# Context times probabilities in a two-layer cross-attention kernel: a 4x3x2 block product of twenty products in place of two Strassen-type halves of eleven

## Chip, core and metric

The kernel runs on one core of a Trainium2 chip, all in float32. The metric is the device time of one execution in microseconds (us); lower is better. TensorE is PE in the profile (PEld is its weight load), VectorE is DVE, ScalarE is ACT, GpSimd is POOL, SyncE is SP, which here only issues transfers.

## What is computed

Eight batches; each has 100 rows `x` (512 wide) and a context of 361 rows (512 wide). Three stages follow one another: a single-head cross-attention (called the first layer below), a block of two 16-head cross-attentions with layer norm in front, and an MLP. Cut to what matters:

```python
# the first layer, per batch
q, k, v = x @ w_q.T, ctx @ w_k.T, ctx @ w_v.T
x = x + alpha * (softmax(q @ k.T / sqrt(512)) @ v) @ w_o.T
# twice, with weights 1 and 2: 16 heads of 128, one more key and value (the bias ones)
h = layer_norm(x)
logits = (h @ wq + bq) @ concat(ctx @ wk + bk, bias_k).T / sqrt(128)     # per head
x = x + (softmax(logits) @ concat(ctx @ wv + bv, bias_v)) @ wo + bo      # per head
# MLP
x = x + gelu(layer_norm(x) @ w_fc1 + b_fc1) @ w_fc2 + b_fc2
```

The kernel doesn't form keys and values. It takes the queries through the key weights to 512 columns ("wide queries", held in the tile `Z`), scores them against the context itself, multiplies the probabilities with the context itself (the *mix*, which overwrites `Z`), and takes that through the value weights (`head_out`). The change concerns the mix: for each batch a matrix of 512 x 361 (the context, transposed by the way PE reads it) times 361 x 1600 (the probabilities of 16 heads x 100 rows).

## The kernel before

**Order.** `emit` walks a list of small units; each issues its instructions in turn, and rings of buffers (`Ring`) issue the loads of weights and contexts as slots come free. A scheduler then settles the order on each engine; every engine works its own queue in order. The mixes, scores, projections and outputs of neighbouring steps are woven into one another by hand (`woven`, `apart`, and the loop at the end of the function), so that PE goes from one to the other while the other engines empty what it has made. `apart` puts two units of the mix that work on the same chunk apart, with another unit between them where it can.

**Steps.** A step is (layer l, pair of batches q, group of heads g), 24 in all, and each has two batches j: 48 *units of work* per execution for the mix. The 1600 probability columns are cut into groups of 576, 512 and 512 (`ROWS`), and each group into two halves of 288 or 256 columns.

**Probabilities.** A pair of score tiles of 128 rows is exponentiated, scaled (ACT, L343) and turned by DVE in blocks of 32 x 32 (`turned`, L359, one instruction for each quarter of the keys and each 32 rows, at a lowered priority) into the tile `pT`. That tile holds nine blocks of 128 keys x half a group: six for the 3 x 2 blocks of probabilities (three blocks of keys, two halves of columns), three for sums of them. When the last quarter of the last pair is turned, `column_sums` (L817) sends the row of the bias key to DRAM and forms the sums on POOL (L822 to L825); in the very last unit on DVE.

**The mix** (`mixed`, L849, matmuls in the helper at L858). The context's 512 columns are four blocks, its 361 rows three (128, 128 and 105). For each half m of the columns there are four parts with eleven products in all, so 22 per unit of work: seven for a 2 x 2 by 2 x 2 product in Strassen's manner, with the accumulators x and z reused from product to product and read in between, and four plain ones for the third block of keys (of 105 rows). The results go into four blocks of `Z` per half: a first value is copied by ACT (L867, L870, L875, L889), three later ones are added by DVE (L878, L884, L885). So a unit of work has eight ACT and six DVE evictions.

**Context blocks.** The 20 stationary blocks of a batch (10 per half) are loaded for each layer into a tile of the ring `ctx` by five transfers (`fill_ctx`, L170 to L179): three from the input, two from a DRAM scratch `cxd`, which holds the 10 summed blocks. These are formed once, in the first layer (`ctx_sums`, L438): five POOL operations of 128 x 256 into the tile `msum` (one buffer) and two transfers out.

**The first layer.** For each batch (`layer0_units`): its context is loaded (`fill_ctx0`, two transfers; rings `ctx` for even and `ctx0` for odd batches, two slots each, so batch b + 4 takes the slot of batch b), transposed for the scores (`ctx_transposed`, which also forms sums in the tile `cT` on DVE, L467 to L469), scored, mixed (`l0_mixed`), summed (`ctx_sums`) and put out. Weights for a bias term (`wqe`) are loaded from POOL's queue (`bias_weights`, L157) and multiplied on DVE (L604) in between. `bias_vectors` (L627) loads two vectors through POOL's queue and subtracts them on DVE.

Of the kernel before, what the change touches and what calls it, by code (L numbers as in the profile page):

```python
# [19 lines left out]
P = 128  # L20
# [23 lines left out]
A11, A12, A22, A13, A23, A33, M1, M2, M3, M4 = range(10)  # L44
# [36 lines left out]
def two_cross_attentions(ctx: ExitStack, tc: tile.TileContext, a: dict, out: bass.AP):  # L81
# [16 lines left out]
    cxd = [dram.tile([P, 10 * P], F32, tag=f"cxd{b}", name=f"cxd{b}") for b in range(B)]  # L98
# [60 lines left out]
    def fill_ctx0(key, t):  # L159
        src = a["ctx_2048"][key[2]]  # L160
        t = t[:, : 3 * D].rearrange("p (k n) -> p k n", k=3)
        nc.sync.dma_start(out=t[:, :2, :], in_=src[: 2 * P].rearrange("(c p) n -> p c n", p=P))
        nc.sync.dma_start(out=t[:TS, 2, :], in_=src[2 * P :])

    def fill_ctx(key, t):
        if key[1] < 0:
            return fill_ctx0(key, t)
        src = a["ctx_2048"][key[2]]
        t = t.rearrange("p (m u n) -> p m u n", m=2, n=P)
        nc.sync.dma_start(out=t[:, :, A11, :], in_=src[:P].rearrange("p (m n) -> p m n", m=2)[:, :, :P])  # L170
        nc.sync.dma_start(
            out=t[:, :, A12:A13, :], in_=src[P : 2 * P].rearrange("p (m u n) -> p m u n", m=2, n=P)
        )
        nc.sync.dma_start(
            out=t[:TS, :, A13:A33, :], in_=src[2 * P :].rearrange("p (m u n) -> p m u n", m=2, n=P)
        )
        d = cxd[key[2]].rearrange("p (m u n) -> p m u n", m=2, n=P)
        nc.sync.dma_start(out=t[:, :, M1:, :], in_=d[:, :, 1:, :])
        nc.sync.dma_start(out=t[:TS, :, A33, :], in_=d[:TS, :, 0, :])  # L179
# [258 lines left out]
    def ctx_sums(b):  # L438

        cx = ctx0(b).rearrange("p k (m u n) -> p k m u n", m=2, n=P)  # L440
        t = work.tile([P, 2, 5, P], F32, tag="pb", name=f"msum_{b}", bufs=1)
        nc.gpsimd.tensor_tensor(t[:, :, 1], cx[:, 0, :, 1], cx[:, 1, :, 1], ALU.add)
        nc.gpsimd.tensor_tensor(t[:, :, 2], t[:, :, 1], cx[:, 0, :, 0], ALU.subtract)
        nc.gpsimd.tensor_tensor(t[:, :, 3], cx[:, 0, :, 1], cx[:, 0, :, 0], ALU.subtract)
        nc.gpsimd.tensor_tensor(t[:, :, 4], cx[:, 1, :, 0], t[:, :, 2], ALU.subtract)
        nc.gpsimd.tensor_tensor(t[:TS, :, 0], cx[:TS, 2, :, 0], cx[:TS, 2, :, 1], ALU.subtract)
        out = cxd[b].rearrange("p (m u n) -> p m u n", m=2, n=P)
        tc.keep_in_program_order(nc.sync.dma_start(out=out[:, :, 1:, :], in_=t[:, :, 1:, :]))
        nc.sync.dma_start(out=out[:TS, :, 0, :], in_=t[:TS, :, 0, :])
# [78 lines left out]
    def layer0_units():  # L528
# [21 lines left out]
        for b in range(B):  # L550
            res.append(unit(lambda b=b: l0_probs(b)))
            res += scored(b + 1)
            res.append(unit(lambda b=b: l0_mixed(b), key0("ctx", b)))
            res.append(unit(lambda b=b: ctx_sums(b), key0("ctx", b)))
            res += turned(b + 2) + normed0(b + 1)
            res += weights(b + 4)
            if b == 0:
                res.append(unit(bias_vectors))
# [258 lines left out]
    def column_sums(l, q, g, j, engine=nc.gpsimd):  # L817


        t, t3 = pTs[l, q, g, j], columns(l, q, g, j)  # L820
        nc.sync.dma_start(out=pbd[l, q * QB + j][:, slice(*ROWS[g])], in_=t3[TS : TS + 1, 2, :])
        engine.tensor_tensor(t[:, 6], t[:, 1], t[:, 0], ALU.subtract)  # L822
        engine.tensor_tensor(t[:, 7], t[:, 3], t[:, 6], ALU.subtract)
        engine.tensor_tensor(t[:, 1], t[:, 1], t[:, 3], ALU.subtract)
        engine.tensor_tensor(t[:, 8], t[:, 2], t[:, 7], ALU.subtract)  # L825
# [10 lines left out]
    def last_turned(l, q, g, j, r, m):  # L836
# [4 lines left out]
        if m:  # L841
            column_sums(l, q, g, j, nc.vector)
# [581 lines left out]
```

## Time and profile before

| | |
|---|---|
| three runs | 1990.54 median (1988.27 to 1991.58) us |
| the profiled execution | 1987.13 us, span 1985.3 us |
| granted PE clock | 0.998 |
| PE busy, mix (tiles mx, mz, my at L858) | 960 + 768 + 384 passes |
| PE busy, 0 to 60 us | 55.3 us |
| PE busy, 60 to 180 us (the first layer's batches) | 111.0 of 120 us |
| PE busy, 180 to 1772 us (the two 16-head layers) | 1569.6 of 1592 us |
| PE busy, 1772 us to the end (last outputs, MLP) | 206.7 of 213.3 us |
| DVE busy, the same four stretches | 13.1, 64.1, 1095.3, 106.7 us |
| POOL busy, the same four stretches | 18.9, 39.1, 580.1, 61.7 us |

A float32 product shows as two matmul instructions (passes), each with its weight load. A pass's listed duration runs into the next one's, since matmuls are pipelined; the pace is read from when the next work starts. In rows of the form `L885 DVE TENSOR_TENSOR Z<-my,Z 128x256 f32<-128x256 f32 x64 | 27.0, 421 | 2.1 <-PE my L858 0.7` the columns are line, engine, operation, output and inputs, shapes, count, busy time in us, mean ns of one, then the idle time just before them and what ended most of it. In tables by stretch the columns are the stretch, its length, and the busy time and count of PE, PEld, DVE, ACT and POOL, then granted clock, share of the transfer engines and GB/s.

### The profile page before, as it was taken

To read this page: it belongs to the slowest core of one execution; us is meant where nothing else is said; L and a number is where in the kernel's file an instruction comes from. 1 tells how busy PE (TensorE), PEld (TensorE's weight loads), DVE (VectorE), ACT (ScalarE), POOL (GpSimd) and SP (SyncE) were. 2 spreads that over 40 slices of the span, in tenths; PEclk is the share of its full clock that TensorE was granted. 3 is DMA by queue.
4 is the path that set the end of the run, shared out by engine and by line. 5 is a ranking of instruction groups with operands and counts; after the bars stand their busy time and mean duration, and the time that the engine had idled before them with its cause. 6 is when DMAs were issued, how large, how long until landed. Compare 5 with 4: busy or idle time off the path is not lost.

```text
span 1985.3 us, 31528 instructions
## 1 busy us (share of the span) xinstructions
PE 1942.6 (98%) x10991; PEld 1788.5 (90%) x10991; DVE 1279.1 (64%) x3555; ACT 761.3 (38%) x2018; POOL 699.8 (35%) x1147
## 2 busy tenths in 40 slices
PE   9999999999999999999999999999999999999999
PEld 5668899999999899999989898999999999889998
DVE  2464776667677677676765766676667677765553
ACT  0324544444442344344433344444433444421331
POOL 3232433543344144525243323333243243325140
PEclk9999999999999999999999999999999999999999
DMA  7696323742545356616533453234234442136432
GB/s 256 243 314 219 99 83 118 243 138 67 189 159 168 108 144 224 206 55 188 173 109 127 120 176 108 86 89 169 89 122 132 128 131 81 58 87 192 125 122 76
DMA packets 250683, 283.90 MB, mean 143 GB/s; under 512 B 37608, under 2 KB 212108, under 8 KB 247196
## 3 DMA queue, kind: packets, MB, share of 16 engines
q1 hardware_dynamic: 246340, 271.51, 43.1%
q0 software_dynamic: 2112, 6.40, 0.9%
q10 hardware_dynamic: 2072, 3.97, 0.6%
q8 instruction: 88, 1.44, 0.3%
q14 instruction: 71, 0.58, 0.1%
HBM read 242.86 MB, written 38.97 MB: 142 GB/s over the span
## 4 chain that ended last, share of the span: by engine, by line
PE 83%; DVE 10%; ACT 3%; DMA 2%; issue 1%; POOL 0%; SPq 0%; DVEq 0%; ACTq 0%
PE sx L748 10%; PE mx L858 9%; PE pq L672 8%; PE mz L858 7%; PE pwo_P L971 7%; PE po L908 7%; PE pqw L688 7%; DVE pT L359 5%; PE sz L748 5%; PE my L858 4%; PE sy L748 2%; PE pgx L1062 2%; PE pfx L1111 2%; PE pfz L1111 1%; PE pgz L1062 1%
## 5 line engine op out<-in xcount | busy, mean ns | idle before, releaser
L359 DVE STREAM_TRANSPOSE pT<-p 32x192 f32<-32x192 f32 (+1 forms) x1664 | 602.2, 362 | 90.9 <-ACT p L343 63.2
L858 PE MATMUL mx<-pT,ctx 128*128 128x256 f32 (+3 forms) x960 | 280.1, 391 | 8.2 <-DVE Z L884 3.1
L748 PE MATMUL sx<-cT,Z 128*128 128x181 f32 x1152 | 225.7, 317 | 2.1 <-DVE p L788 2.1
L782 POOL TENSOR_SCALAR p<-nsb 128x1 f32<-128x1 f32 x192 | 38.1, 217 | 499.1 <-DVE pT L359 441.2
L858 PE MATMUL mz<-pT,ctx 105*128 105x256 f32 (+3 forms) x768 | 206.1, 390 | 7.5 <-ACT Z L870 4.1
L748 PEld LDWEIGHTS sx<-cT,Z 128*128 128x128 f32 x1152 | 193.2, 190 | 13.7 <-DVE p L788 3.6
L672 PE MATMUL pq<-hT,wq 128*128 128x200 f32 x1024 | 194.5, 335 | 2.2 <-DMA wq<-in_L_xattn_wq_dram 2.2
L688 PE MATMUL pqw<-q,wkT 128*128 128x200 f32 x1024 | 194.4, 333 | 0.6 <-ACT q L680 0.6
L908 PE MATMUL po<-Z,wv 128*128 128x200 f32 x1024 | 194.8, 335 | 0.0
L858 PEld LDWEIGHTS mx<-pT,ctx 128*128 128x128 f32 (+1 forms) x960 | 169.4, 189 | 24.9 <-DVE Z L884 7.1
L802 ACT ACTIVATE p<-p,nm 128x362 f32<-128x362 f32 x192 | 114.7, 597 | 179.9 <-DVE nm L801 176.6
L672 PEld LDWEIGHTS pq<-hT,wq 128*128 128x128 f32 x1024 | 177.3, 191 | 6.9 <-issue 3.2
L688 PEld LDWEIGHTS pqw<-q,wkT 128*128 128x128 f32 x1024 | 176.2, 189 | 7.1 <-ACT q L680 1.4
L908 PEld LDWEIGHTS po<-Z,wv 128*128 128x128 f32 x1024 | 176.2, 191 | 5.0 <-issue 1.0
L858 PEld LDWEIGHTS mz<-pT,ctx 128*128 128x128 f32 (+1 forms) x768 | 144.2, 190 | 40.2 <-ACT Z L870 8.2
L801 DVE TENSOR_REDUCE nm<-p 128x1 f32<-128x362 f32 x192 | 101.5, 529 | 112.4 <-ACT p L793 102.7
L731 POOL TENSOR_TENSOR sums<-Z 128x256 f32<-128x256 f32 x96 | 70.8, 737 | 229.7 <-ACT Z L691 135.5
L691 ACT COPY Z<-pqw 128x400 f32<-128x400 f32 x256 | 122.4, 489 | 73.8 <-PE pqw L688 73.3
L748 PE MATMUL sz<-cT,sums 128*128 128x181 f32 x768 | 149.5, 316 | 0.0
L343 ACT ACTIVATE p<-p,rden 128x362 f32<-128x362 f32 (+2 forms) x216 | 129.0, 598 | 34.6 <-DVE rden L342 34.5
L748 PEld LDWEIGHTS sz<-cT,sums 128*128 128x128 f32 x768 | 124.7, 189 | 0.1
L858 PE MATMUL my<-pT,ctx 128*128 128x256 f32 (+3 forms) x384 | 102.6, 388 | 0.0
(385 smaller groups left out, 3095.5 us busy)
## 6 DMA issues: line engine op xcount, KB each, us to landing
wv<-in_L_xattn_wv_dram SPq DMA_DIRECT2D x64, 512.0 KB
wq<-in_L_xattn_wq_dram SPq DMA_DIRECT2D x64, 512.0 KB
wkT<-wkd SPq DMA_DIRECT2D x48, 512.0 KB
cT<-cTd SPq DMA_DIRECT2D x16, 1267.0 KB
wo_S<-wod SPq DMA_DIRECT2D x32, 512.0 KB
f<-in_L_xattn_w_fc_dram SPq DMA_DIRECT2D x32, 512.0 KB
wo_A<-in_L_xattn_wo_dram SPq DMA_DIRECT2D x24, 512.0 KB
xr<-xd SPq DMA_DIRECT2D x45, 200.0 KB
```

What stands on the lines that cost most here:

```text
L343: nc.scalar.mul(p[:rows, :n], p[:rows, :n], rden[:rows])
L359: nc.vector.transpose(dst[keys, :, :, i, :], src[i * QD : (i + 1) * QD, :, :, quarter, :])
L672: nc.tensor.matmul(ps, w[:, c, (h % 2) * K : (h % 2 + 1) * K], hTs[l, q][:, c, :], start=(c == 0), stop=(c == DT - 1),)
L688: nc.tensor.matmul(ps[:, c, :], w[:, h % 2, cc * P : (cc + 1) * P], qs[h], start=True, stop=True)
L691: nc.scalar.copy(Z[:, 2 * c2 : 2 * c2 + 2, :, h * L : (h + 1) * L], ps.rearrange("p c (b t) -> p c b t", b=QB),)
L731: nc.gpsimd.tensor_tensor(t[:, 0], a2[:, :2, :], a2[:, 2:, :], ALU.add)
L748: nc.tensor.matmul(ps[:, :KH], st["a"][a][:, c, :], st["ct"][:, blk, c, :], start=(first and c == 0), stop=(c == 1), skip_group_check=not ...
L801: nc.vector.tensor_reduce(nm, p[:, :S1], AX.X, ALU.max, negate=True)
L802: nc.scalar.activation(p[:, :S1], p[:, :S1], AF.Exp, bias=nm, accum_out=den)
L858: nc.tensor.matmul(ps, cx[:w, blk, :], pT[:w, u, :], start=first, stop=last, skip_group_check=more)
L908: nc.tensor.matmul(ps, w[:, c, (h % 2) * K : (h % 2 + 1) * K], Z[:, c, :, h * L : (h + 1) * L], start=(c == 0), stop=(c == DT - 1),)
L971: nc.tensor.matmul(ps, w[:, h, :], OB[i, j][:, h, :], start=(h == 0 and not more), stop=(h == 7), skip_group_check=more)
```

## The change

The mix of a unit of work becomes one product of a 4 x 3 matrix of context blocks with a 3 x 2 matrix of probability blocks in 20 products, written as tables. `MIX` has ten parts of two products, one per *lane* (an accumulator in PSUM); an entry is (lane, opens a fresh accumulator, context block, probability block, (result, factor) pairs). Where a lane isn't opened, the product is accumulated on what the lane holds, which has been read before. Every block has 128 keys now; the context's rows past 361 are zeros.

```diff
+TURN_SUMS = (
+    (0, 9, 1, 5, "-"),
+    (0, 15, 0, 2, "-"),
+    (0, 7, 0, 1, "-"),
+    (0, 10, 7, 2, "-"),
+    (0, 8, 3, 10, "+"),
+    (0, 12, 9, 8, "+"),
+    (1, 14, 3, 5, "-"),
+    (1, 11, 1, 4, "-"),
+    (1, 6, 4, 5, "-"),
+    (1, 13, 3, 6, "+"),
+    (1, 5, 0, 4, "-"),
+    (1, 0, 2, 13, "-"),
+)
+MIX = (
+    (
+        (0, True, 4, 9, ((7, 1),)),
+        (1, True, 5, 15, ((0, 1),)),
+    ),
...
+    (
+        (0, True, 15, 4, ((2, 1), (3, 1))),
+        (1, False, 18, 8, ((3, 1), (5, 1))),
+    ),
+)
...
+    def mix_slots(l, q, g, j):
+        r0, r1 = ROWS[g]
+        h, t = (r1 - r0) // 2, pTs[l, q, g, j]
+        places = [Z[:, m, j, r : r + h] for m in range(DT) for r in (r0, r0 + h)]
+        return [t[:, u] for u in range(9)] + places
...
+    def column_sums(l, q, g, j):
+        slots = mix_slots(l, q, g, j)
+        for e, i, x, y, sign in TURN_SUMS:
+            (nc.vector, nc.gpsimd)[e].tensor_tensor(slots[i], slots[x], slots[y], ALU.add if sign == "+" else ALU.subtract)
...
+    def mixed(l, q, g, j, part):
+        cx = rings["ctx"].tiles["ctx", l, q * QB + j].rearrange("p (u n) -> p u n", n=P)
...
+        for lane, opens, u, v, results in MIX[part]:
+            if opens:
+                lanes[lane] = psum(ps_mm, [P, h], f"m{'xz'[lane]}_{l}_{q}_{g}_{j}_{part}")
+            ps = lanes[lane]
+            nc.tensor.matmul(ps, cx[:, u, :], slots[v], start=opens, stop=True, skip_group_check=True)
+            for o, f in results:
+                key, dst = (l, q, g, j, o), slots[9 + o]
+                if key not in begun:
+                    begun.add(key)
+                    nc.scalar.mul(dst, ps, float(f)) if f != 1 else nc.scalar.copy(dst, ps)
+                elif abs(f) == 1:
+                    nc.vector.tensor_tensor(dst, dst, ps, ALU.add if f == 1 else ALU.subtract)
```

The twelve sums of probabilities are split over DVE (first entry 0) and POOL (1); seven of them lie in the unit's own eight result places of `Z`, which are free by then, and are overwritten as the results arrive. They are formed after the last quarter, whose order changes from 0, 1, 2, 3 to 3, 0, 1, 2; the bias key's row goes out after quarter 3. The 14 later values of a unit of work are added by DVE, the eight first ones come through ACT. `apart` now parts any two units of one mix.

The twenty context blocks are formed in the first layer by 24 operations on 128 x 128 (`CTX_SUMS`: 16 on POOL, one of them a multiplication by -1; eight on DVE, where both signs are negative), in part in place, in the context's own tile, and ten in `more` (the old `msum` buffer, now of ten blocks). All twenty are written to `cxd`, and one transfer loads them for each later layer.

```diff
     def fill_ctx0(key, t):
...
+        nc.gpsimd.memset(t[96:, 2, :], 0.0)
         nc.sync.dma_start(out=t[:, :2, :], in_=src[: 2 * P].rearrange("(c p) n -> p c n", p=P))
-        nc.sync.dma_start(out=t[:TS, 2, :], in_=src[2 * P :])
+        nc.sync.dma_start(out=t[:96, 2, :], in_=src[2 * P : 2 * P + 96])
+        nc.sync.dma_start(out=t[96:TS, 2, :], in_=src[2 * P + 96 :])
     def fill_ctx(key, t):
...
+        nc.sync.dma_start(out=t, in_=cxd[key[2]])
...
     def ctx_sums(b):
+        t = rings["ctx0" if b % 2 else "ctx"].tiles["ctx", -1, b]
+        more = work.tile([P, 10, P], F32, tag="pb", name=f"msum_{b}", bufs=1)
...
+        for i, f, x, g, y in CTX_SUMS:
+            if g == 0:
+                nc.gpsimd.tensor_scalar(block(i), block(x), -1.0, 1.0, ALU.mult, ALU.mult)
+            elif f == g == -1:
+                nc.vector.scalar_tensor_tensor(block(i), block(x), -1.0, block(y), ALU.mult, ALU.subtract)
+            else:
+                x, y = (x, y) if f == 1 else (y, x)
+                nc.gpsimd.tensor_tensor(block(i), block(x), block(y), ALU.add if f == g else ALU.subtract)
+        out = cxd[b].rearrange("p (u n) -> p u n", n=P)
+        nc.sync.dma_start(out=out[:, 8:18, :], in_=more)
+        nc.sync.dma_start(out=cxd[b][:, : 8 * P], in_=t[:, 12 * P : 20 * P])
+        for k, i in enumerate(CTX_ALSO):
+            nc.sync.dma_start(out=out[:, 18 + k, :], in_=block(i))
```

`bias_vectors` moves ahead of the first batch's `ctx_sums`.

## Prediction

> **What bounds the kernel now.** First the busy shares and the 40 slices, to see which engine carries the span and whether its spare time is spread evenly.
>
> ```profile
> PE 1942.6 (98%) x10991; PEld 1788.5 (90%) x10991; DVE 1279.1 (64%) x3555; ACT 761.3 (38%) x2018; POOL 699.8 (35%) x1147
> ...
> PE   9999999999999999999999999999999999999999
> ...
> DVE  2464776667677677676765766676667677765553
> ```
>
> PE is full in every slice. DVE stands at 60 to 70% through the middle, so it is the next engine, and an average hides where it is fuller. I therefore cut the trace into the 47 stretches between one group's first column sum (L822) and the next group's, 207.9 to 1772.3 us: each holds one mix, one set of scores and their transposes. Two short stretches and a long one (length, then PE, weight load, DVE, ACT, POOL busy):
>
> ```profile
> 292.94:319.83 26.89, 26.37 (x148) 24.76 (x147) 21.80 (x59) 12.49 (x34) 11.85 (x24) 1.00 0.37 97
> 487.43:513.95 26.52, 25.41 (x141) 23.78 (x140) 20.17 (x56) 12.49 (x34) 18.19 (x32) 1.00 0.40 103
> 1148.93:1183.88 34.95, 34.95 (x208) 33.18 (x207) 21.12 (x58) 14.34 (x38) 6.78 (x13) 1.00 0.48 158
> ```
>
> In the long one DVE works 60% of the time and PE never stops. In the short ones DVE works 81% and 76%, and PE already loses 0.5 and 1.1 us. Of the 47, 15 are shorter than 30 us (mean 27.75 us, DVE 20.66), 32 are longer (mean 35.88, DVE 23.86). Last, the price of a product, from the timeline of PE, and of the vector work, from the groups split by shape and from one line's own view:
>
> ```profile
> 899.76 1.03 PE L858 MATMUL mz<-pT,ctx 128*128 128x256 f32 x4
> 900.63 0.78 PE L748 MATMUL sx<-cT,Z 128*128 128x181 f32 x4
> ...
> L885 DVE TENSOR_TENSOR Z<-my,Z 128x256 f32<-128x256 f32 x64 | 27.0, 421 | 2.1 <-PE my L858 0.7
> L885 DVE TENSOR_TENSOR Z<-my,Z 128x288 f32<-128x288 f32 x32 | 14.3, 448 | 3.7 <-PE my L858 3.4
> L1020 DVE TENSOR_TENSOR Z<-O,Z 128x400 f32<-128x400 f32 x8 | 4.6, 569 | 1.2 <-ACT O L1071 1.2
> L1024 DVE TENSOR_TENSOR fs<-fs,f 128x1024 f32<-128x1024 f32 x4 | 4.9, 1220 | 0.1
> L705 POOL TENSOR_TENSOR both<-Z x16: 452/460/647, 167.8 to 1610.6; 128x128 f32<-128x128 f32 x16
> ```
>
> Four passes begin at 899.76 and the next work at 900.63: 0.217 us a pass, though one is listed as lasting 0.385 (they overlap). A product is two passes.
>
> **The products.** 48 units (2 layers, 8 batches, 3 groups) lose two products each; the changed order of instructions has 5645 matmuls where there were 5741, that is 96 fewer. 32 units are 256 wide: 32 x 4 passes x 0.217 = 27.8 us. 16 are 288 wide, a pass 0.217 x 288/256 = 0.244: 16 x 4 x 0.244 = 15.6. Together 43.4 us, 0.9 us a unit. PE has no idle time to swallow them, so this is the whole gain on offer.
>
> **The evictions.** ACT keeps eight per unit. Two of them now multiply by -1; the nearest rows are the ACT copy of 128x256 at 0.37 us and the ACT operation with an operand of 128x200 at 0.42 to 0.45, so between 0 and 0.15 us x 96 = 14 us. ACT is 38% busy and I take 0. DVE goes from 6 to 14 per unit: 8 x (2 x 0.418 + 0.452)/3 = 3.4 us more a unit. They read PSUM and one SBUF operand, as the rows do, so I see no second price.
>
> **The sums of probabilities.** Four POOL operations become six on POOL and six on DVE. A DVE sum with both inputs in SBUF is not in the trace at this width. Between 400 and 1024 columns the rows rise by (1.22 - 0.57)/624 = 1.04 ns a column, so 0.42 us at 256, 0.45 at 288, mean 0.43: 2.6 us a unit. That is the lower bound. But POOL's six run at the same moment, and there the trace shows a price:
>
> ```profile
> L467 DVE TENSOR_TENSOR cT_-1_3_537<-cT_-1_3_537 128x362 f32<-128x362 f32 x1 | 0.5, 537 | 0.0
> L467 DVE TENSOR_TENSOR cT_-1_4_632<-cT_-1_4_632 128x362 f32<-128x362 f32 x1 | 0.8, 781 | 0.0
> ...
> 99.45 0.95 DVE L468 TENSOR_TENSOR cT_-1_4_632<-cT_-1_4_632 128x362 f32<-128x362 f32 x1
> ...
> 98.99 1.02 POOL L443 TENSOR_TENSOR msum<-msum,ctx_-1_3_230 128x256 f32<-128x256 f32 x1
> ```
>
> Beside POOL the same sums take 0.78 to 1.06 us for 0.53, and POOL 1.02 for 0.72: a factor of about 1.75 on DVE. In the changed DVE order one of the six stands alone and five follow the last transposes, where POOL does its own: 0.43 + 5 x 0.75 = 4.2 us. The upper bound is that each waits for a whole POOL operation (0.73): 6 x (0.43 + 0.73) = 7.0. So DVE gains 3.4 + 4.2 = 7.6 us a unit, between 6.0 and 10.5.
>
> A rule speaks against the change here. The Trainium skill, "SBUF — State Buffer", section "Who interferes with whom", says that a DVE instruction with two SBUF inputs and a GpSimd instruction that reads SBUF share a port that one of them holds until it ends. By it the sum would be the upper bound; the rows above show less than a full lock, about 0.4 us of waiting where POOL's operation takes 0.7.
>
> **DVE against PE, stretch by stretch.** In the 15 short stretches DVE would need 20.66 + 7.6 = 28.3 us where PE needs 27.75 - 0.9 = 26.9; in the 32 long ones 23.86 + 7.6 = 31.5 where PE needs 35.0. DVE is in order, and each of its mix evictions is followed by a product into the same PSUM tile: a lane's accumulation waits 13 times a unit instead of 8. So a DVE behind its time stops PE, and what DVE gains in a long stretch is not handed back. No stretch shows DVE above 81%, so how full it can get is unknown: 1.00 at best, and at 0.81 PE already loses up to 4%; I bound it by 0.90 and take 0.95. With each stretch as long as the larger of (its length - 0.9) and (DVE + 7.6)/0.95, the sum over the 47 is 12.8 us more than now, 23 of them set by DVE. At 6.0 and 1.00 it is 36 less; at 7.6 and 1.00, 17 less; at 7.6 and 0.90, 58 more; at 10.5 and 0.95, 100 more. I take +13.
>
> **The first layer.** Per batch, five POOL sums of 128x256 (3.6 us) become 16 POOL operations of 128x128 (x 0.45 = 7.2 us) and 8 DVE ones (0.29 to 0.38 in the L604 rows, 2.7 us), in one chain that changes engine. POOL already waits here for the transfer out of the one msum buffer, and the 16 transfer engines are full from 70 to 180 us:
>
> ```profile
> 78.75 0.72 POOL L442 TENSOR_TENSOR msum<-ctx_-1_1_227 128x256 f32<-128x256 f32 x1 [12.10 <-DMA cxd<-msum]
> ...
> 60.00:180.00 120.00, 111.01 (x658) 87.69 (x657) 64.10 (x255) 35.17 (x101) 39.14 (x61) 0.99 0.86 293
> ```
>
> Blocks written out double from 10 to 20 of 65.5 KB a batch, 5.2 MB in all: at 293 GB/s 18 us of a queue that is 86% busy. Two new waits sit in front of other work. POOL clears the tail of a new context tile (a memset) before its load, and that waits for the old tile's writes out; behind it on POOL are the wqe loads, rstd and the next sums. On DVE, multiplications by -1 of a later batch stand ahead of this batch's cT sums, which PE's scores need. SP issues four writes out instead of two and three loads instead of two per batch ahead of cTd and the weights. One batch now takes 12.1 us from sums to sums; chain 7.2 + 2.7, a few changes of engine and 3 to 6 us for the landing make some 14. Bounds: 0, hidden behind other work, to the 18 us of transfers plus 8 x 3 of chain, 42. I take 8 x 1.5 = 12.
>
> **The drain and the rest.** In the last unit the old order weaves two chunks of products; the new has two lanes, each waiting for its eviction: 0.43 us of the other lane against about 0.9 us (0.27 from PE's end to DVE, 0.42, and back), some 0.4 x 8 = 3 us; 0 to 5. Main-stage context loads go from five transfers to one (16 loads, 64 SP issues fewer at 0.5 to 0.9 us); nothing waits for SP there, so 0, as for the bias row sent a quarter earlier. If the mix waited for its block, one would cost the landing, some 4 us.
>
> Sum: 13 + 12 + 3 = 28 us on the profiled run's own 1987.1 (span 1985.3 and 1.8 around it): 2015. The three runs shown have their median at 1990.5, 3.4 higher, which I leave inside the range.
>
> **The rivals.** *PE stays the bound* (faster): the sums hardly meet POOL's and transposes fill every gap. For it: DVE runs transposes back to back and PE waits only 7 us for evictions of the mix now. Against it: eight more of them in a queue with no slack in the short stretches. -36 to -17, first layer 5, drain 1: 1957 to 1976, say 1966; the kernel gains at all while DVE's addition stays below about 6.2 us at 0.95, where the main stage's -15 meets the 15 elsewhere. *Full alternation of DVE and POOL* (slower still): 10.5 us a unit, +100 + 12 + 3 = 2102, decided if a DVE sum takes above 1 us. Against it is the 1.75 above. *The first layer alone*: main stage -17, first layer 30, drain 3: 2003, if PE's losses sit before 200 us.
>
> **Chances.** Forecast 0.48 (1990 to 2050), PE-bound 0.26, alternation 0.14, first layer 0.12. Two measurements of this kernel are told apart by about 0.2%, 4 us. Faster 0.26, from the PE-bound case and a sliver of the last; within 0.2% 0.07, from the low edge of the forecast; slower 0.67. The range that leaves out half of the alternation and the best of the PE-bound case is 1960 to 2085; the forecast's own is 1990 to 2050.
>
> **What would show it.** Right: DVE at 80% or more of the span, PE below 97%, waits of PE for DVE's Z additions at tens of us, DVE sums at 0.7 to 0.8 us, the same 47 stretches longer where they were short. Wrong: PE at 98% and a span shorter by 30 us; or PE's new idle time all before 200 us.

## The result, and the profile after

The changed kernel takes 2090.57 us (median of four runs, 2085.79 to 2091.43) where the kernel before, run beside it, took 1989.4: a ratio of 1.0505, 95% interval 1.0483 to 1.0527. It is slower by some 101 us. The prediction had 2015 and a range up to 2085: the sign was right, the size was not. The profiled execution has a span of 2089.6 us against 1985.3, 104.3 more.

The page of the changed kernel, the lines that answer to those shown of before (busy us, share of the span, instructions; then 40 slices):

```profile
PE 1948.0 (93%) x10799; PEld 1761.9 (84%) x10799; DVE 1596.4 (76%) x4291; ACT 752.7 (36%) x2018; POOL 853.5 (41%) x1339
...
PE   7987889999999989999999999999999999889999
...
DVE  2483789788889789888887878788878888886543
```

PE executes 192 passes less and is busy 5 us longer: it has gaps now, and the work behind a gap is listed longer. Its waits between 200 and 1890 us, by what ended them (total us, times, longest):

```profile
PE mx L957 <- DVE Z L921: 19.8, 16, 2.6
PE mx L957 <- DVE Z L964: 16.8, 22, 2.4
PE sx L836 <- DVE p L876: 15.7, 13, 1.7
PE mz L957 <- ACT Z L962: 14.7, 13, 1.4
PE mz L957 <- DVE Z L964: 10.3, 21, 1.2
```

They are spread over several causes: sums of probabilities (L921), evictions of the mix (L964, L962), and the additions of the scores (L876), which the change didn't touch. The groups of L921 and L964 on DVE, split by shape:

```profile
L964 DVE TENSOR_TENSOR Z<-Z,mx 128x256 f32<-128x256 f32 x256 | 100.9, 413 | 18.7 <-PE mx L957 16.5
...
L964 DVE TENSOR_TENSOR Z<-Z,mz 128x256 f32<-128x256 f32 x192 | 77.3, 415 | 4.4 <-PE mz L957 1.9
...
L921 DVE TENSOR_TENSOR Z<-pT 128x256 f32<-128x256 f32 x96 | 55.5, 578 | 1.7
...
L921 DVE TENSOR_TENSOR pT<-pT 128x256 f32<-128x256 f32 x32 | 27.1, 847 | 0.0
```

All evictions of L964 together are 274 us, 151 more than the mix's on DVE before; all DVE sums of L921 are 197 us for 288, 0.685 us each.

To see where 104.3 us go, I cut every span at the start of POOL's first and last sum named `both` (16 of them in either kernel, one per layer and batch). Up to the first is the *first layer*, between them lies the *stage*, most of the two 16-head layers, and behind them the *tail*: the last six units of work of the mix, the drain and the MLP.

| | first layer | stage | tail |
|---|---|---|---|
| before | 167.8 | 1442.8 | 374.7 |
| after | 196.3 | 1503.3 | 390.0 |
| difference | +28.5 | +60.5 | +15.3 |

The forecast for first layer, stage and drain was +12, +13 and +3, but by other cuts: at each group's first sum of probabilities on POOL (L822 before, L921 after). By those the first layer ends at 207.9 us before and 239.4 after (+31.5), the 47 stretches between the sums take 1564.4 and 1632.2 us together (+67.7), and from the last of them to the end it is 213.0 and 218.1 us (+5.1). The 15 short stretches grew from 27.75 to 30.86 us in the mean, with DVE busy 26.61 us of it (86%), the 32 long ones from 35.88 to 36.54, with DVE busy 30.10 us (82%).

In what follows, *first layer*, *stage* and *tail* are the parts of the table. The expectations of three early runs speak of a 16-head stage of 1667 us, a longer cut; there the first layer and the totals are to be compared.

### The profile page after: what moved, and what is told of

The parts are those of the page before. It is cut to its first block, busy times and chain, and to the rows that moved or that the text cites. A ratio compares the mean times of both kernels' runs of the same rounds, so it can differ in the third digit from the quotient of the medians.

```text
span 2089.6 us, 32367 instructions
## 1 busy us (share of the span) xinstructions
PE 1948.0 (93%) x10799; PEld 1761.9 (84%) x10799; DVE 1596.4 (76%) x4291; ACT 752.7 (36%) x2018; POOL 853.5 (41%) x1339
## 4 chain that ended last, share of the span: by engine, by line
PE 44%; DVE 34%; ACT 5%; issue 5%; POOL 3%; DMA 3%; DVEq 0%; SPq 0%; POOLq 0%; ACTq 0%
DVE pT L436 16%; PE mz L957 5%; DVE Z L964 5%; PE mx L957 5%; PE pwo_P L1048 5%; PE sx L836 5%; PE po L985 4%; PE pq L760 4%; PE pqw L776 4%; DVE Z L921 3%; PE pgx L1139 2%; PE pfx L1188 2%; PE sz L836 2%; DVE pT L921 2%; ACT p L890 2%
## 5 line engine op out<-in xcount | busy, mean ns | idle before, releaser
L436 DVE STREAM_TRANSPOSE pT<-p 32x192 f32<-32x192 f32 (+1 forms) x1664 | 602.1, 362 | 57.1 <-ACT p L420 28.0
L836 PE MATMUL sx<-cT,Z 128*128 128x181 f32 x1152 | 230.4, 320 | 18.7 <-DVE p L876 15.7
L957 PE MATMUL mz<-pT,ctx 128*128 128x256 f32 (+1 forms) x672 | 207.8, 395 | 16.8 <-DVE Z L964 9.6
L985 PE MATMUL po<-Z,wv 128*128 128x200 f32 x1024 | 196.3, 335 | 0.0
L957 PE MATMUL mx<-Z,ctx 128*128 128x256 f32 (+1 forms) x480 | 155.3, 406 | 34.4 <-DVE Z L921 19.8
L964 DVE TENSOR_TENSOR Z<-Z,mx 128x256 f32<-128x256 f32 (+1 forms) x384 | 155.3, 424 | 30.8 <-PE mx L957 27.9
L957 PEld LDWEIGHTS mz<-pT,ctx 128*128 128x128 f32 x672 | 124.7, 191 | 51.4 <-DVE Z L964 18.1
L921 POOL TENSOR_TENSOR Z<-pT 128x256 f32<-128x256 f32 (+1 forms) x144 | 133.7, 941 | 69.3 <-DVE pT L436 48.4
L957 PE MATMUL mx<-pT,ctx 128*128 128x256 f32 (+1 forms) x480 | 149.5, 394 | 6.0 <-DVE Z L964 4.8
```

Source lines behind the costliest of these rows:

```text
L436: nc.vector.transpose(dst[keys, :, :, i, :], src[i * QD : (i + 1) * QD, :, :, quarter, :])
L836: nc.tensor.matmul(ps[:, :KH], st["a"][a][:, c, :], st["ct"][:, blk, c, :], start=(first and c == 0), stop=(c == 1), skip_group_check=not ...
L921: (nc.vector, nc.gpsimd)[e].tensor_tensor(slots[i], slots[x], slots[y], ALU.add if sign == "+" else ALU.subtract)
L957: nc.tensor.matmul(ps, cx[:, u, :], slots[v], start=opens, stop=True, skip_group_check=True)
L964: nc.vector.tensor_tensor(dst, dst, ps, ALU.add if f == 1 else ALU.subtract)
L985: nc.tensor.matmul(ps, w[:, c, (h % 2) * K : (h % 2 + 1) * K], Z[:, c, :, h * L : (h + 1) * L], start=(c == 0), stop=(c == DT - 1),)
```

## Experiments: the first layer

Already the first scores of PE start 9.2 us later, at 56.27 us for 47.07. The timeline of DVE in the changed kernel (start, duration, engine, line, operation, in brackets the idle time before and what ended it):

```profile
23.91 1.02 DVE L529 SCALAR_TENSOR_TENSOR ctx_-1_0_221<-ctx_-1_0_221 128x128 f32<-128x128 f32 x4 [23.91 <-DMA ctx_-1_0_221<-in_ctx_dram]
28.79 1.02 DVE L529 SCALAR_TENSOR_TENSOR ctx_-1_1_231<-ctx_-1_1_231 128x128 f32<-128x128 f32 x4 [3.86 <-DMA ctx_-1_1_231<-in_ctx_dram]
29.73 3.93 DVE L485 COPY O<-px 128x400 f32<-128x400 f32 x8
```

and that of PE:

```profile
30.35 24.35 PE L491 MATMUL pq<-O,Z 128*128 128x400 f32 x64 [7.35 <-DVE O L485]
```

Context sums (L529) that wait for a transfer stand at the head of DVE's queue, the copies of x behind them, and PE waits 7.35 us for those copies. The first run pins the eight sums where the program has them.

```diff
-                nc.vector.scalar_tensor_tensor(block(i), block(x), -1.0, block(y), ALU.mult, ALU.subtract)
+                tc.keep_in_program_order(nc.vector.scalar_tensor_tensor(...))
```

> The changed kernel with the eight DVE operations of each batch's context sums held in program order on DVE; nothing else. The first POOL sum of the 16-head stage for a new batch (line `both`) starts at 196.3 us in the changed kernel and at 167.8 in the one before, 28.5 late. Theory Q (queue order: DVE stands still for a context load that the work behind it doesn't need): the 9 us lost before the first scores go, and with them part of the 19 lost over the eight batches, so 172 to 185 us and a total of some 2066 to 2080. Rival C (the chain of 24 operations and the doubled transfers set the pace): only the 9 go at most, 187 or later, total 2080 or more.

2091.04 us, ratio 1.0504 (1.0473 to 1.0536). The first scores start at 46.7 us, so the wait is gone, but the first `both` comes at 198.8 us: the 9 us are lost again further on. The wait was real and didn't set the end.

The second leaves the 24 sums out and keeps the transfers.

```diff
-        for i, f, x, g, y in CTX_SUMS:
+        for i, f, x, g, y in ():
...
-        nc.sync.dma_start(out=out[:, 8:18, :], in_=more)
+        nc.sync.dma_start(out=out[:, 8:18, :], in_=t[:, : 10 * P].rearrange("p (u n) -> p u n", n=P))
...
```

> The changed kernel with the arithmetic of the context sums left out: the same number of bytes of unsummed blocks goes to the scratch, and the later layers read them. Rival C by its chain, or theory Q: the start of the 16-head stage goes back to 168 to 173 us. If the transfers (5.2 MB more written, a third load, the wait of the memset) set the first layer, it stays at 180 or later. The 16-head stage itself (1667 us) should not move by more than 5.

2064.91 us, 1.0373 (1.033 to 1.0416). The first layer takes 169.9 us, 26.4 of the 28.5 less. Without the arithmetic the doubled transfers cost 2 us; the rest goes with it. The third makes all 24 on DVE, pinned, so that the chain doesn't change engine.

```diff
-                nc.gpsimd.tensor_tensor(block(i), block(x), block(y), ALU.add if f == g else ALU.subtract)
+                ins = nc.vector.tensor_tensor(block(i), block(x), block(y), ALU.add if f == g else ALU.subtract)
+            tc.keep_in_program_order(ins)
```

> All 24 operations of a batch's context sums on DVE and in program order, so the chain has no change of engine and POOL does none of it: 24 x 0.29 = 7 us of DVE a batch, 56 in all, in a stretch where DVE is busy 62 of 105 us. Theory H (the hand-overs between POOL and DVE, each of them blocking one queue, cost the first layer its 28 us): the 16-head stage starts at 172 to 184 us, total 2065 to 2078. Rival W (the amount of vector work in the chain): 190 or later.

2078.53 us, 1.0446 (1.0406 to 1.0486), first layer 183.7: 12.6 of the 28.5 us go with POOL's share of the chain and its hand-overs, 15.9 stay (the pinning by itself had brought nothing).

## Experiments: what the sums of probabilities cost

If DVE is simply too full, its six sums a unit belong on POOL (41% busy), and twelve on DVE must be worse. If they come too late, the mix must begin later.

```diff
# run 1                                      # run 2
+ nc.gpsimd.tensor_tensor(slots[i], ...)     + nc.vector.tensor_tensor(slots[i], ...)
# run 3
-                lead = (len(part) + 2) // 3 if ahead else len(part) - 2 + j
+                lead = (len(part) + 2) // 3 + 2 if ahead else len(part) - 2 + j
```

> All twelve sums of probabilities of a unit on POOL, none on DVE: DVE loses 4.1 us a unit (197 us in all) and the two engines no longer meet over them, POOL gains 6 x 0.74 = 4.4 us a unit. Theory D (DVE's load costs PE its time): the 16-head stage goes from 1667 us to 1600 to 1630, total 2025 to 2055. Rival S (the mix starts late because its sums are late): the chain of twelve on POOL takes some 9 us where the split one takes 5 to 6, and the stage stays or grows, 1667 to 1720, total 2090 or more.

> All twelve sums of probabilities of a unit on DVE, none on POOL: DVE gains 6 x 0.42 us and loses some 6 x 0.27 of meeting POOL, so 0.9 to 1.5 us more a unit; POOL loses 4.6; the chain of sums takes 12 x 0.42 = 5 us, about as long as the split one, but with no change of engine. Theory D: the stage from first to last `both` grows from 1503 to 1515 to 1560. Theory S (when the last sums are ready counts, and what stands behind them on POOL): 1470 to 1500.

> The changed kernel with each mix begun two units of work later within its step. Theory S: the waits of PE for the sums (19.8 us for DVE's, 14.7 for the first copies) fall under 10, and the stage goes from 1503 to 1475 or less. Theory D: the waits only move, 1495 to 1525.

All three are slower than the change: 2114.55 us (1.0622, stage 1528.0), 2160.76 (1.0859, stage 1570.3) and 2137.54 (1.0742, stage 1538.1). With the sums on POOL two of PE's waits are

```profile
PE mz L957 <- ACT Z L962: 56.0, 27, 3.3
PE mx L957 <- POOL Z L921: 22.5, 17, 3.6
```

that is, for sums and for results whose place still holds a sum that another sum has to read. With twelve on DVE its share between 300 and 1700 us is 83.6%, as in the change (83.0%). With the later mix the waits for sums are gone and those for evictions and scores have grown. The last two lie above both ranges that had been expected. None of the three hypotheses is enough alone. So I took the parts away one by one: the sums (the products read unsummed blocks), and then the lanes as well (each product on a fresh accumulator).

```diff
-        for e, i, x, y, sign in TURN_SUMS:
+        for e, i, x, y, sign in ():
...
-            if opens:
+            if True:                        # second run only
...
-            nc.tensor.matmul(ps, cx[:, u, :], slots[v], start=opens, stop=True, skip_group_check=True)
+            nc.tensor.matmul(ps, cx[:, u, :], slots[v % 6], start=opens, stop=True, skip_group_check=True)
```

> The sums of probabilities are left out (the products read the unsummed blocks instead), so DVE loses 4.1 us and POOL 4.6 us a unit; evictions and lanes stay. Theories D and S both: the 16-head stage falls to 1565 to 1600 us, since DVE is then at 72% or the mix can begin at once, total 1990 to 2025. Rival E (the 14 evictions and 13 lane waits alone hold PE): it stays at 1630 us or more.

> The sums of probabilities left out as in e4_nosums, and each of the twenty products opens a fresh accumulator, so no product waits until its lane has been read (the accumulation is left out with it); the 22 evictions stay. From the first to the last sum `both`, the 16-head stage took 1442.8 us before, 1503.3 in the changed kernel and 1438.0 without the sums, where the 40 us of products alone would make it 1403. Theory L (the remaining 35 us are lane waits): 1400 to 1415, total 1970 to 1990. Theory D (they are the load of 14 evictions on DVE, which delays scores and transposes too): 1428 or more, total 2000 or more.

Without sums 2010.32 us (1.0099), stage 1438.0, tail 374.8 as before the change. Without lanes too 1988.23 (0.9995, 0.9981 to 1.0009), stage 1417.9, between the ranges of the two theories. Taken off in this order, the sums cost 65.3 us of the stage and all of the tail's loss, the lanes 20.1. Next, sums that nobody reads, in the change as it is; the bare products with six DVE evictions a unit; and the change with three operands replaced so that no sum reads a place of the result.

```diff
# sums unread
+            i = 8 if e else 6 + n % 2
+            (nc.vector, nc.gpsimd)[e].tensor_tensor(slots[i], slots[x % 6], slots[y % 6], ...)
# products only (on top of no sums, fresh accumulators)
-                elif abs(f) == 1:
+                elif part in (3, 6, 7) and abs(f) == 1:
# places unread
-    (0, 8, 3, 10, "+"), (0, 12, 9, 8, "+"), (1, 0, 2, 13, "-"),
+    (0, 8, 3, 7, "+"), (0, 12, 1, 8, "+"), (1, 0, 2, 6, "-"),
```

> All twelve sums of probabilities are formed, six on VectorE and six on GpSimd as in the change, but nothing reads them: they go to the spare places behind the probabilities, every input is an unsummed block, and the products read unsummed blocks (so the output is not the reference's). The engines' load is that of the change; no product, copy or sum waits for a sum. Without the sums the stage from the first batch's context sum on GpSimd to the last one was 1438.0 us, with them 1503.3. Theory D, pure load (VectorE is too full and the sums push everything else on it back): 1485 to 1503 us, total 2065 to 2092. Theory W, waits for the sums' values and for the places they sit in: 1438 to 1460 us, total 2010 to 2035. In between the two share the 65 us.

> The main stage as bare as it gets: no sums of probabilities, each product on a fresh accumulator, and of the fourteen additions of a unit that VectorE makes only six left, as many as before the change (the other results' additions are left out, so the output is not the reference's). The same kernel with all fourteen had a stage of 1417.9 us and 1988.2 us in all. If the eight further evictions a unit cost the remaining 15 us, the stage is 1400 to 1406 us (the 1442.8 of before less 43.4 for 192 matrix passes = 1399.4) and the total 1970 to 1978; if they cost nothing and the products are simply worth less than 43 us, the stage stays at 1414 to 1420 us and the total at 1985 to 1990.

> The change with three operands replaced: sums 8, 12 and 0 read block 7, 1 or 6 instead of the sums 10, 9 and 13 that lie in places of the result, so no sum reads a place into which a result is copied later (the values of these sums are others, so the output is not the reference's). Count, engines and order of all operations stay. In the change ScalarE's first copy of a result waited 29.8 us in 16 units for VectorE's last sum, which reads the place that it writes. If this wait behind a place in use sets the pace, the stage falls from 1503.3 us to 1475 to 1490 and the total to 2060 to 2077, and the waits of PE for ScalarE's copies (14.7 us) nearly vanish. If VectorE's load does, the wait goes but the stage stays within 5 us of 1503 and the total within 2083 to 2094.

Unread sums: 2117.59 us (1.0662), stage 1526.9, above what either theory gave. So the sums cost no less when nobody waits for their values. Places unread: 2103.94 (1.0578), stage 1510.3, above both ranges too. ACT's waits for DVE's sums in front of its copies, 29.8 us in the change, are gone, and the stage is no shorter: the wait behind a place in use isn't it either. Products only: 1964.2 us (0.988, 0.986 to 0.9901), stage 1398.1, 2 us below the 1400 to 1406 expected. PE's busy time in the stage falls from 1422.8 to 1380.8 us, so the 192 passes are worth their 43.4 us but for 1.4. The eight further evictions a unit cost 1417.9 - 1398.1 = 19.8; with them PE's waits of the mix for the transposes (L436) go from 2.2 to 16.8 us.

That left DVE's load. If load is what counts, the sums must be cheaper on a DVE that has the eight evictions less.

```diff
-        for e, i, x, y, sign in ():
+        for e, i, x, y, sign in TURN_SUMS:          # on top of products only; read
```

> The twelve sums of probabilities are formed and read as in the change, but each product takes a fresh accumulator, and VectorE makes six of the fourteen additions of a unit (the other results' additions are left out, so the output is not the reference's). Without the sums this kernel had a stage of 1398.1 us and a total of 1964.2. Theory A, the sums have a price of their own (values that come late, GpSimd beside them): they cost what they did on the full VectorE, 65 us, stage 1455 to 1470 us, total 2035 to 2055 with some 15 at the end. Theory D, price by how full VectorE is: the stage of 1417.9 us with fourteen additions and no sums had 3.15 us of VectorE more a unit, the sums bring 4.1, so they cost 20 to 32 us, stage 1418 to 1430, total 1985 to 2005; and the same operations are dearer only behind the eight further additions.

2054.3 us (1.0334), stage 1474.0: 75.9 us, not 20 to 32, and a little above theory A too. The theory of a full DVE fell here, and with it the reasoning of the prediction: DVE is busy 72% of the span in this run, as in the one with fourteen additions and no sums, whose stage is 56 us shorter. The two halves of the sums by themselves, read by nobody, and the best version so far with the sums at a lower priority:

```diff
+        for n, (e, i, x, y, sign) in enumerate(TURN_SUMS):
+            if e == 0:                              # the other run: e == 1
+                i = 8 if e else 6 + n % 2
+                ...tensor_tensor(slots[i], slots[x % 6], slots[y % 6], ...)
# third run, on top of the context sums on DVE
+        with tc.high_priority(offset=-60):
```

> The kernel without sums, with fresh accumulators and six VectorE additions a unit (stage 1398.1 us, total 1964.2), and in it only the six sums of VectorE, read by nobody; the six of GpSimd are left out (the output is not the reference's). With all twelve sums, read, the stage was 1474.0. Theory V, what costs is VectorE's time in its queue, 2.6 us a unit at 0.43 us a sum when GpSimd is not beside it: stage 1420 to 1450. Theory P, what costs is GpSimd beside VectorE: VectorE's sums alone cost little, stage 1398 to 1412. If most of it is the values arriving late, both halves unread cost little and this stays under 1410 too.

> As the run before, but with only the six sums of GpSimd, read by nobody, and those of VectorE left out (the output is not the reference's). Theory V: GpSimd has room (30% busy without the sums, 41% with them) and nothing of VectorE's is added, so the stage stays at 1398 to 1412 us. Theory P: GpSimd's sums hold up what stands behind them on its own queue (the scores' operand sums, the biases) or slow VectorE's operations, and the stage rises to 1430 to 1465 by itself.

> The best version so far that computes the reference (the change with the context sums all on VectorE, 2078.5 us, stage 1501.8), with the twelve sums of a unit given a priority 60 instructions lower, so that the order of VectorE lets evictions of scores and of the mix pass in front of them. If the sums cost what they hold up behind them, the stage falls to 1465 to 1490 us and the total to 2042 to 2068; if values then come late, or the sums are spread already, it stays at 1495 to 1515 or gets worse.

DVE's half alone: 2032.98 us (1.0218), stage 1462.9, +64.8, above the range of theory V. POOL's half alone: 1965.64 (0.9879), stage 1396.6: nothing. The lower priority: 2087.92 (1.0495), stage 1510.8, no help: PE's waits for DVE's sums come to 23.4 us there and those for the additions of the scores to 19.3, where the change had 19.8 and 15.7. So DVE's six sums carry the price, on a DVE that has time for them. The timeline of DVE in the run with DVE's half shows where they stand:

```profile
901.23 6.13 DVE L436 STREAM_TRANSPOSE pT<-p 32x192 f32<-32x192 f32 x16 [0.67 <-ACT p L420]
907.40 0.43 DVE L994 SCALAR_TENSOR_TENSOR O<-po,vecs,pb 128x200 f32<-128x200 f32 x1
907.74 2.81 DVE L923 TENSOR_TENSOR pT<-pT 128x256 f32<-128x256 f32 x5
910.48 0.33 DVE L871 TENSOR_TENSOR p<-sz,p 128x180 f32<-128x180 f32 x1
910.73 0.41 DVE L994 SCALAR_TENSOR_TENSOR O<-po,vecs,pb 128x200 f32<-128x200 f32 x1
911.07 0.33 DVE L876 TENSOR_TENSOR p<-sx,p 128x180 f32<-128x180 f32 x1
```

and that of PE at the same time:

```profile
906.90 0.78 PE L836 MATMUL sy<-cT,Z 128*128 128x181 f32 x4
907.52 0.66 PE L959 MATMUL mx<-pT,ctx 128*128 128x256 f32 x2
908.02 0.59 PE L959 MATMUL mz<-pT,ctx 128*128 128x256 f32 x2
911.45 0.88 PE L836 MATMUL sx<-cT,Z 128*128 128x181 f32 x4 [2.84 <-DVE p L876]
```

Sixteen transposes hold DVE for 6.1 us; PE has work until 908.6, just beyond them. The five sums follow behind one other operation, 2.8 us, and PE, whose next scores need an accumulator that L876 has to empty, stops for 2.84 us. Over the whole run (200 to 1890 us) these waits come to twice those of products only, and a second kind is larger still: there the five sums stand in front of L674, which empties the accumulators of the transposed rows behind a layer norm. Products only:

```profile
PE sx L836 <- DVE p L876: 10.3, 11, 2.2
PE psb L730 <- DVE hT L674: 0.3, 1, 0.3
```

DVE's half, with one such place on DVE and on PE:

```profile
PE sx L836 <- DVE p L876: 20.8, 16, 2.8
PE mz L959 <- DVE hT L674: 13.2, 4, 3.8
PE mx L959 <- DVE hT L674: 6.4, 2, 3.5
PE psb L730 <- DVE hT L674: 3.2, 2, 3.0
...
740.49 4.16 DVE L923 TENSOR_TENSOR pT<-pT 128x256 f32<-128x256 f32 x5
744.57 0.87 DVE L674 TENSOR_SCALAR hT<-ph,vec_b 128x200 f32<-128x200 f32 x2
...
745.10 0.70 PE L959 MATMUL mz<-pT,ctx 128*128 128x256 f32 x2 [3.58 <-DVE hT L674]
```

Of the 64.8 us, 42 are idle time of PE in the stage (59.4 us where products only has 17.2), the rest a longer busy time for the same passes (1403.5 us for 1380.8).

Before that reading was put to the test, one more attempt at a better kernel: all sums on POOL, the mix begun one or two units of work later, the context sums on DVE.

```diff
+            nc.gpsimd.tensor_tensor(slots[i], slots[x], slots[y], ...)
+                lead = (len(part) + 2) // 3 + 2 if ahead else len(part) - 2 + j     # second run: + 1
```

> GpSimd's six sums of probabilities cost nothing when nobody waits for them, VectorE's six cost 65 us. So here all twelve are GpSimd's, each mix begins two units of work later so that they are ready, and the context sums of the first layer are VectorE's. Alone, the sums on GpSimd gave a stage of 1528.0 us, where PE waited 78.5 us for results and sums that were late, and the later mix alone gave 1538.1, where it waited for VectorE instead. If the two causes are these, they cancel: stage 1440 to 1475 us, total 2005 to 2045. If beginning the mix later costs by itself (the mix is packed more closely into what is left of a unit's time, and its evictions with it), the stage stays above 1490 and the total above 2060.

> The same with the mix begun one unit of work later instead of two. If lateness is what counts, it lies between the 1528.0 us of no lead and the run before: stage 1465 to 1500 us, total 2030 to 2065. If packing counts, it is faster than the run before.

2064.29 us (1.0386, 1.0368 to 1.0403), stage 1487.2, and 2068.49 (1.0406), stage 1493.6. The first is the fastest version that leaves nothing out, and 3.9% slower than before. Its stage lies between the two ranges that had been expected, and the second is slower than it, as lateness had it, inside that range by the stage and 3 us above it by the total. In the first, PE's waits for sums are gone from the list of the largest, those for evictions of the mix (23.3 and 12.7 us for DVE, 18.7 for ACT) aren't. What exactly the later mix costs was not taken apart.

The last run changes the place of DVE's six sums: two at a time, half a unit later, between the row maximum and the reciprocal. (The last unit's six aren't made, 282 of 288 are; that lies behind the stage.)

```diff
         nc.scalar.activation(p[:, :S1], p[:, :S1], AF.Exp, bias=nm, accum_out=den)
+        for _ in range(min(2, len(late))):
+            tc.keep_in_program_order(nc.vector.tensor_tensor(*late.pop(0)))
...
+                late.append((slots[6 + n % 2], slots[x % 6], slots[y % 6], ...))
```

> VectorE's six sums alone, read by nobody, as in the run that had a stage of 1462.9 us and a total of 2033.0 (64.8 us in the stage above the same kernel without them, 1398.1). There five of the six stand in VectorE's order right behind the last transposes of a unit and in front of the additions of the next scores. Here the same six are formed half a unit later, two at a time, pinned between the row maximum and the reciprocal of a later block of rows, where VectorE waits 0.8 us for ScalarE's exponential anyway (the output is not the reference's, as there). Place theory: the stage is 1398 to 1425 us, the total 1964 to 1993. Load theory (what VectorE has to do counts, wherever it stands): the stage is 1450 to 1475 and the total 2020 to 2045.

1972.18 us (0.9906, 0.9875 to 0.9936), stage 1402.9, inside the ranges of the place theory. Of the 64.8 us that DVE's half cost, 60.0 are gone: PE idles 19.5 us of the stage, and its waits for L876 and L674 are 12.6 and 0.6 us. Its DVE timeline, where L895 are the sums:

```profile
881.46 6.13 DVE L436 STREAM_TRANSPOSE pT<-p 32x192 f32<-32x192 f32 x16 [0.67 <-ACT p L420]
887.62 0.43 DVE L999 SCALAR_TENSOR_TENSOR O<-po,vecs,pb 128x200 f32<-128x200 f32 x1
887.97 0.34 DVE L871 TENSOR_TENSOR p<-sz,p 128x180 f32<-128x180 f32 x1
888.22 0.42 DVE L999 SCALAR_TENSOR_TENSOR O<-po,vecs,pb 128x200 f32<-128x200 f32 x1
888.55 0.34 DVE L876 TENSOR_TENSOR p<-sx,p 128x180 f32<-128x180 f32 x1
888.80 0.34 DVE L877 TENSOR_TENSOR p<-sy,p 128x181 f32<-128x181 f32 x1
889.18 0.53 DVE L891 TENSOR_REDUCE nm<-p 128x1 f32<-128x362 f32 x1
889.62 0.75 DVE L895 TENSOR_TENSOR pT<-pT 128x256 f32<-128x256 f32 x2
890.52 0.16 DVE L419 RECIPROCAL rden<-den 128x1 f32<-128x1 f32 x1
```

The scores' additions follow the transposes directly, and the sums lie where DVE waited for ACT's exponential. DVE's own waits for ACT say the same. Products only, without sums:

```profile
DVE rden L419 <- ACT p L890: 86.5, 115, 0.9
DVE nm L889 <- ACT p L881: 76.3, 62, 2.7
DVE pT L436 <- ACT p L420: 65.0, 97, 2.2
```

the sums behind the transposes:

```profile
DVE rden L419 <- ACT p L890: 88.4, 114, 1.7
DVE nm L889 <- ACT p L881: 72.6, 65, 2.7
DVE pT L436 <- ACT p L420: 60.5, 95, 1.3
```

the sums spread:

```profile
DVE nm L891 <- ACT p L881: 63.1, 54, 2.7
DVE pT L436 <- ACT p L420: 62.7, 97, 1.6
...
DVE rden L419 <- ACT p L892: 15.4, 31, 0.8
```

Behind the transposes the sums leave these waits as they were: DVE works 150 us more (1440.6 for 1290.8) and idles as long in the softmax chain. Spread, they take the place of 71 us of waiting for the exponential. The sums themselves are shorter too: 121.5 us for 282, 0.43 each, against 168 for 288, 0.58. So the place brings back both the stall and some 43 us of DVE's time (the 46 between these rows less the six sums that aren't made); how the 60 us divide between the two was not tried.

DVE's share between 300 and 1700 us beside the stage shows how little a share tells:

| kernel | DVE share | stage |
|---|---|---|
| before | 68.1% | 1442.8 (with 192 passes more) |
| products only | 70.1% | 1398.1 |
| DVE's sums behind the transposes | 76.0% | 1462.9 |
| DVE's sums spread | 76.8% | 1402.9 |
| eight more evictions, no sums | 77.7% | 1417.9 |
| the change | 83.0% | 1503.3 |

## Why the prediction was wrong

**Right: the prices of the instructions.** The products' 43.4 us are there (1398.1 where 1442.8 - 43.4 = 1399.4). DVE's evictions rose by 151 us / 48 = 3.15 us a unit for 3.4 forecast, its sums take 197 / 48 = 4.1 for 4.2. Together that is 7.25, but DVE's busy time rose by only 6.15 us a stretch (in the timelines a row often begins before the one ahead of it ends). ACT's multiplications by -1 were taken at 0; their rows have 382 ns against 369 for the copy at 256 columns, some 1.3 us in all. The first of the named signs, DVE at 80% of the span, came out at 76% (83% between 300 and 1700 us) and DVE's sums at 0.685 us, just under the 0.7 to 0.8; PE below 97%, tens of us of waits for Z, and short stretches that grow came true (46.6 of the 67.7 us lie in the 15 short ones).

**Wrong: a stretch as long as "the larger of (its length - 0.9) and (DVE + 7.6)/0.95".** The prediction turned 7.6 us a unit into time through DVE's share of each stretch, and so gave +13. Measured between the same sums it is +67.7. With the stretches paired in order, the 23 that the rule let DVE set were to grow by 34.4 us together and grew by 46.2; the 24 that it left to PE were to shrink by 21.6 and grew by 21.5. So most of the miss lies where by the rule DVE had room. The runs showed that an instruction on DVE has no price by share here: 3.15 us a unit of evictions cost 19.8 us, 3.5 us a unit of sums behind the transposes cost 64.8, and 2.6 us of the same sums in the exponential's gap 4.8, all with DVE at 76 to 78%. Where it had noted that five sums "follow the last transposes", it used the fact for their duration beside POOL, and not for what they hold up: the additions of the next scores and L674. That place makes the price was shown in the kernel with products only, with sums that nobody reads; that it makes the 65.3 us in the change too is inferred from that, and the lower priority there did not confirm it.

The prediction's bound of 0.90 gives +58, near the measured number, but by luck: with the 6.15 us that DVE really gained a stretch the same rule gives some +15 at 0.90 and some -17 at 0.95. Its own rows spoke against a price by share: PE lost 1.1 us in the short stretch with DVE at 76% and 0.5 in the one at 81%, so "at 0.81 PE already loses up to 4%" joins the loss of the one to the share of the other.

**Named and not priced: the lanes.** "a lane's accumulation waits 13 times a unit instead of 8" stood in the text without a term of its own. It is 20.1 us (1438.0 - 1417.9).

**First layer, +12 for +28.5** (+31.5 up to the first sum of probabilities). Inside its bounds of 0 to 42, and the doubled transfers, 18 us of the upper one, are 2 us. The term that was mis-sized is the chain of 24 operations: 26.4 us, of which 12.6 go when it stays on one engine. Multiplications ahead of other work in DVE's queue, which the prediction named, did come, at the first loads, and pinning them brought nothing.

**Drain, +3 for +5.1.** By its own cut the prediction is close, at the edge of its 0 to 5. The tail's +15.3 is larger because it begins earlier: 10.2 of it (161.7 to 171.9 us) lie between the last `both` and the last unit's sums, in units like those of the stage. Without sums the tail is 374.8 us, as before.

**The rivals.** "PE stays the bound" fell with PE at 93% of the span, "The first layer alone" with 67.7 of the 104.3 us in the stretches. "Full alternation of DVE and POOL" had 2102 us, near the result, but its deciding point, a DVE sum above 1 us, isn't reached (0.685). The Trainium skill's rule in "SBUF — State Buffer", "Who interferes with whom" (an operation of VectorE with two inputs in SBUF contends with one of GpSimd that reads SBUF, for a port that one of them holds alone), has the right direction: the sums take 0.43 us in the gaps, 0.58 without POOL's sums and 0.685 beside them, where a full turn would be 1.16. It is part of the price and doesn't make it: POOL's sums beside products only cost nothing, and beside DVE's, with the values read, 1474.0 - 1462.9 = 11.1 us.

Parts of the stage: products -44.7, evictions +19.8, lanes +20.1, sums +65.3, together +60.5. They add up because they are the steps of one chain of runs; in another order they differ (the sums cost 75.9 us on top of products only), and the first step also leaves out the four sums of before and its reuse of accumulators.

## What to carry to other kernels

An instruction added to a busy in-order engine cost by where it stood: behind a long block and ahead of what the bounding engine waits for, 168 us of sums cost 64.8 us; in a gap of the engine's own chain 121.5 us of them cost 4.8, at the same share. So look, in the timeline, for what stands behind the new instructions, before working with averages; and where a scheduler decides, pin them into the waits that the engine has anyway. A saved product was worth its passes only where all that it needs was left out: the ceiling here was 1.2% (products only). Whether all of it can find such places is open: a version that reads the sums from the better place, with a mix begun late enough, was not tried.

## What was not expected of the hardware

PE loses more than its gaps. 192 passes fewer left PE's busy time at 1948.0 us for 1942.6; in the stage the same passes are busy 1380.8 us with products only and 1419.9 in the change. A gap is followed by passes listed longer (0.88 us for four passes of sx behind a wait, 0.78 without). The granted clock is 0.998 before, 0.991 with products only, 0.985 in the change and 0.978 with unread sums. It doesn't follow PE's idle time alone: with all sums on POOL and the mix two units later PE idles 113 us of the span at 0.992, with DVE's half 106 us at 0.985. How much of the longer busy time is the clock was not taken apart.
